# Four graph layers on one core: the queries of the last two layers through a replicated DRAM table, the lock of the slow work released, the row fetch of layer 0 moved

## The chip, the core and the metric

The kernel runs on one core of a Trainium2 chip. The metric is the device time of one execution in microseconds (us). Every time below comes from the runs of the kernel before or from one profiled execution of it.

## The reference, cut to what matters

Sixteen graphs share one adjacency matrix of 1024 nodes with about 8 neighbours for each node. Node features are 128 numbers in float32. Four layers follow each other; layers 0, 2 and 3 are attention with 8 heads of 16 numbers, layer 1 is a graph attention with one head.

```python
# layers 0, 2, 3
Q = (h @ Wq); K = (h @ Wk); V = (h @ Wv)          # 8 heads of 16
scores = einsum(Q, K) / 4, -inf where adj == 0
attn_out = softmax(scores) @ V
x = layer_norm(h + attn_out @ Wo + bo)
x = layer_norm(x + relu(x @ W1 + b1) @ W2 + b2)
# layer 1
h = x @ W;  e = leaky(h @ a_src [:, None] + h @ a_dst [None, :]), -inf where adj == 0
x = layer_norm(softmax(e) @ h + x)
```

## The kernel before, in words

Nodes are sorted by their number of neighbours, and the sparse rows are gathered. The 16 graphs are handled as two groups `g` of eight, and each group as two halves `h` of four. A **unit** is a layer `l`, a group `g` and a tile `t` of 128 sorted nodes; there are 4 x 2 x 8 = 64 units, run in that order. For each unit the neighbours are taken in rounds: a chunk is 32 nodes with four neighbours each, on 128 partitions, so a gathered row sits on partition 32 s + n for neighbour s of node n. Two chunks (in layer 1 four) make a **part**. In layers 0, 2 and 3 the units t = 0 to 7 have 10, 6, 6, 6, 4, 4, 4 and 3 parts; in layer 1 they have 6, 3, 3, 3, 2, 2, 2 and 2.

One part i of an attention layer passes through these functions:

- `gathered` (L750): indirect DMAs from POOL fetch table rows (keys and values of eight graphs, 8 KB a row) into `e`. Four buffers exist, and parts are fetched three ahead.
- `products` (L761): DVE multiplies keys by `qr`, the queries of the unit repeated on all four groups of 32 partitions.
- `exponentials` (L777, L781): DVE sums over each head, ACT takes the exponential.
- `weighted` (L802): DVE multiplies values by `ex`.
- `summed` (L829): PE adds the neighbours up into `acc`.
- `divided` (L843 to L861), at a unit's end: sums of exponentials, reciprocal, division; it appends two **tails**, one for each half.

A tail (`attention_tail`, `graph_tail`) runs the rest of the layer for 128 nodes of four graphs: output projection, two normalizations (`normed`, with ACT L502 and L511 and the power on POOL L508), the feed-forward part, and `finish`. In `finish` the result is turned (`turned`, L518) into `xn`, stored to the DRAM tensor `kept`, and projected by `project` to the table rows of the next layer (L460, L464, store L469; into layer 1 L480 to L495). Tails are Python generators; each `yield` is a point where other work can be placed.

Every engine runs its instructions in the order in which the Python program emits them; a hand-written schedule sets it. The main loop emits one part after the other and calls `others()` three times for a part (four times in layer 1). A call advances the tails at a pace of `STEPS` steps for a unit (`GRAPH_STEPS` after layer 1), and one step of `fronts`, or, if that is empty, of `slow`:

- `fronts` holds `queries(u + 1)` and `loaded(u + 2)`, put there at the second part of a unit and used up by its end. `queries` multiplies x by Wq (L722), copies the result to `q` (L726), repeats it on the four groups of partitions by matmuls with the constant `rep` (L731), and copies it to `qr` (L734). `qr` has two buffers. `loaded` fetches x for the unit after next: from `kept` on SP's queue, in layer 0 by an indirect DMA of `in_x` (L693) and a transposition (L518).
- `slow` holds `at_leisure(1)`: the projection of group 1 of the input for layer 0, 16 tiles `xg` of 128 nodes and four graphs. It has to be done before unit (0, 1, 0) is gathered.

`finish` and `at_leisure` both use the two `xT` buffers, and two flags keep them apart. `busy` counts tails that are in `finish`; `held` is true while `at_leisure` is within a tile. `finish` begins with

```python
            while held[0]:
                advance(slow)
```

and `at_leisure` sets `held[0] = False` after a tile and then goes straight on to the next one, where it sets `held[0] = True` before its next `yield`.

Weights of the next attention layer are loaded at the start of the unit t = 1 of group 0 (`load_weights`, two sets of buffers). SP issues all DMAs that are not indirect, in program order; POOL issues the indirect ones.

Of the kernel before, what the change touches and what calls it, by code (L numbers as in the profile page):

```python
# [12 lines left out]
F32 = mybir.dt.float32  # L13
# [7 lines left out]
P = 128  # L21
D = 128
# [20 lines left out]
GR = 2  # L43
# [17 lines left out]
            CHUNK[_t, _r, _j] = len(CHUNK)  # L61
NC = len(CHUNK)

STEPS = 15
GRAPH_STEPS = 9
AHEAD = 3

# [9 lines left out]
def sparse_path(ctx: ExitStack, tc: tile.TileContext, a: dict, out: bass.AP, flag):  # L77
# [358 lines left out]
    for l, (_, names) in enumerate(LAYERS):  # L436
# [5 lines left out]
        (l, g): dram.tile([T, P, HF, GH * P], F32, name=f"kept{l}{g}")  # L442
        for l in range(1, len(LAYERS)) for g in range(GR)
    }
    xs = {}
    srcs = {}


    def project(l, g, t, h, x, kv=None):

        if l:
            nc.sync.dma_start(kept[l, g][t, :, h, :], x.rearrange("p g n -> p (g n)"))
        table = tables[l, g][t * P : (t + 1) * P, :]
        if LAYERS[l][1] is ATTN:
            if kv is None:
                kv = twos.tile([P, 2, GH, D], F32, tag="kv", name="kv")
            for i in range(0, GH, 2):
                ps = bank([P, 2, 2 * D])
                for k in range(2):
                    nc.tensor.matmul(  # L460
                        ps[:, k, :], x[:, i + k, :], w[LAYERS[l][0], "Wkv"],
                        start=True, stop=True,
                    )
                nc.scalar.copy(  # L464
                    kv[:, :, i : i + 2, :].rearrange("p c g d -> p g c d"),
                    ps.rearrange("p g (c d) -> p g c d", d=D),
                )
                yield
            nc.sync.dma_start(  # L469
                table.rearrange("p (c x) -> p c x", c=2)[:, :, h * GH * D : (h + 1) * GH * D],  # L470
                kv.rearrange("p c g d -> p c (g d)"),
            )
            return
        kv = twos.tile([P, GH * D + GH], F32, tag="kv", name="kv")
        if h == 0:
            srcs[g, t] = const.tile([P, G], F32, name=f"src{g}{t}")
        for i in range(0, GH, 2):
            ps = bank([P, 2, D + 2])
            for k in range(2):
                nc.tensor.matmul(ps[:, k, :], x[:, i + k, :], wg, start=True, stop=True)  # L480
            nc.scalar.copy(
                kv[:, i * D : (i + 2) * D].rearrange("p (g d) -> p g d", d=D), ps[:, :, :D]
            )
            to = GH * D + i
            nc.scalar.copy(
                kv[:, to : to + 2].rearrange("p (g o) -> p g o", o=1), ps[:, :, D : D + 1]
            )
            at = h * GH + i
            nc.scalar.copy(
                srcs[g, t][:, at : at + 2].rearrange("p (g o) -> p g o", o=1), ps[:, :, D + 1 :]  # L490
            )
            yield

        nc.sync.dma_start(table[:, h * GH * D : (h + 1) * GH * D], kv[:, : GH * D])
        nc.sync.dma_start(table[:, ROW + h * GH : ROW + (h + 1) * GH], kv[:, GH * D :])  # L495
# [31 lines left out]
    def finish(l, g, t, h, z, gain, shift):  # L527
        if l + 1 < len(LAYERS):

            while held[0]:  # L530
                advance(slow)
            busy[0] += 1
            xn = states.tile([P, GH, P], F32, tag="xT", name="xT")
            turned(z, xn, gain, shift)
            yield
            yield from project(l + 1, g, t, h, xn)
            busy[0] -= 1
            return
        o = twos.tile([P, GH, D], F32, tag="kv", name="outs")
        nc.gpsimd.tensor_tensor(o, z, over_graphs(gain), ALU.mult)  # L540
        nc.gpsimd.tensor_tensor(o, o, over_graphs(shift), ALU.add)
        nc.gpsimd.indirect_dma_start(
            out=out.rearrange("n (k c) -> (n k) c", k=GR * HF),
            out_offset=bass.IndirectOffsetOnAxis(ap=places[:, g, h, t : t + 1], axis=0),
            in_=o.rearrange("p g d -> p (g d)"), in_offset=None,
        )
# [66 lines left out]
        at = (g * HF + h) * GH * D  # L613
        return slice(at, at + n * GH * D)

    busy, held = [0], [False]

    def at_leisure(g):
        def fetch(k):
# [10 lines left out]
        for k in range(T * HF):  # L630
# [4 lines left out]
            yield  # L635
            yield from steps
            held[0] = False

    def at_once(g):

# [40 lines left out]
    def loaded(u):  # L681
# [5 lines left out]
        if l == 0:  # L687
            for h in range(HF):
# [6 lines left out]
                    in_=a["x"].rearrange("n (k c) -> (n k) c", k=GR * HF),  # L695
                    in_offset=bass.IndirectOffsetOnAxis(ap=places[:, g, h, t : t + 1], axis=0),
                )
                yield
                turned(rows, xs[units[u]][:, h])
            yield  # L700
            return
# [5 lines left out]
    def queries(u):  # L707

        l, g, t = units[u]
        if not is_attention(u):  # L710
# [4 lines left out]
            nc.scalar.copy(ofs[u], ps)  # L715
            return
        qs[u] = reps.tile([P, J, ROW], F32, tag="qr", name="qr")
        for h in range(HF):
            q = ones_.tile([P, GH * D], F32, tag="q", name="q")
            ps = bank([P, GH, D])  # L720
# [143 lines left out]

    tails = []
    fronts = []
    slow = []

    def advance(gens):
# [9 lines left out]
    def others():  # L879
        pace[0] += pace[1]  # L880
        while pace[0] >= 1.0:
            advance(tails)
            pace[0] -= 1.0
        for gens in (fronts or idle(),):
            if gens and next(gens[0], "end") == "end":
                gens.pop(0)

    with tc.manual_schedule():
        wide = [gather_buffer() for _ in range(AHEAD + 1)]
# [34 lines left out]
        for i in range(len(parts) + 1):  # L924
# [30 lines left out]
                pace[:] = 0.0, steps / (passes * sum(part[0] == u for part in parts) - 1)  # L955
            if here and u + 1 < len(units):
                if i == begun + 1:
                    fronts.append(queries(u + 1))
                    fronts.append(loaded(u + 2))
                    if units[u + 2 : u + 3] and units[u + 2][0]:  # L960
                        for _ in fronts.pop():
                            pass
            others()
            if here and is_attention(u):
                exponentials(i)
# [450 lines left out]
```

## Time and profile before

| | |
|---|---|
| median of 3 runs | 2901.22 us (2899.43 to 2903.95) |
| profiled execution, its own time | 2907.46 us |
| its span in the profile | 2905.7 us |
| busy: PE, DVE, ACT, POOL | 72%, 71%, 50%, 53% |
| DMA moved | 611.00 MB, 210 GB/s |
| queue q0 (indirect), q1 (SP) | 485.12 MB, 123.51 MB |
| layer 0, layer 1 (from the first part) | 96 to 956 us, 956 to 1349 us |
| layer 2, layer 3 | 1349 to 2094 us, 2094 us to the end |

Stages are read from the timeline of DVE: a unit begins with its first `products` (L761), in layer 1 with its first L783. In a line of waits the columns are the waiting instruction, what it waited for, the sum in us, how often, and the longest. In a line of the timeline they are start, duration, engine, line, operation and shapes, and in brackets the idle time of the engine ahead of it and what ended that. A busy share is a mean over stages with different limits, so the windows by stage matter more than the totals.

### The profile page before, as it was taken

The numbers are of one execution on the slowest core, as the hardware profiler recorded it, in microseconds if no ns is written. First come the engines' busy times: TensorE is split into PE (matmuls) and PEld (weight loads), VectorE is DVE, ScalarE is ACT, GpSimd is POOL, SyncE is SP. The second block draws the span as 40 slices with busy tenths as digits, with TensorE's granted clock in tenths as the row PEclk, the third lists the DMA queues.
The fourth block names the chain that finished last, engine by engine and source line by source line (L and its number), as shares of the span: only waits on it lengthen the run. The fifth ranks groups of instructions, "written<-read, shape, count | busy, mean of one in ns | idle before, by whom it ended". The sixth has DMA issues, their size and how long they took to land.

```text
span 2905.7 us, 35508 instructions
## 1 busy us (share of the span) xinstructions
PE 2101.5 (72%) x12692; PEld 1310.9 (45%) x12692; DVE 2076.4 (71%) x1416; ACT 1458.6 (50%) x4578; POOL 1542.7 (53%) x1096
## 2 busy tenths in 40 slices
PE   6456777777777867766578877887777776757666
PEld 5334544444454534333245544554544444334444
DVE  7872585678776566667788659886688876888771
ACT  3133555644566545445256664556645455435554
POOL 3342354354554687784254334544346767586773
PEclk8687888887798988888688998889988788887787
DMA  7656464357464577787567546675566554366540
GB/s 248 249 194 213 158 240 164 135 189 271 166 258 141 194 275 270 267 288 290 194 235 264 193 176 253 237 266 192 186 235 229 199 218 168 140 249 213 189 146 20
DMA packets 168842, 611.00 MB, mean 210 GB/s; under 512 B 44600, under 2 KB 47672, under 8 KB 120158
## 3 DMA queue, kind: packets, MB, share of 16 engines
q0 software_dynamic: 100736, 485.12, 46.4%
q1 hardware_dynamic: 67920, 123.51, 11.6%
q8 instruction: 102, 1.67, 0.2%
q14 instruction: 84, 0.69, 0.1%
HBM read 654.67 MB, written 92.34 MB: 257 GB/s over the span
## 4 chain that ended last, share of the span: by engine, by line
PE 26%; POOL 13%; ACT 11%; DVE 9%; issue 8%; DMA 3%; POOLq 0%; SPq 0%; DVEq 0%; ACTq 0%
POOL e L750 6%; PE ps L572 5%; PE yps L581 4%; PE acc L829 4%; POOL rstd L508 4%; DVE sc L777 3%; ACT z L502 3%; PE ps L518 3%; DMA e<-table,idx 2%; ACT qr L734 2%; DVE pr L802 2%; PE yps L585 2%; PE ps L460 2%; DVE pr L761 2%; PE yps L562 2%
## 5 line engine op out<-in xcount | busy, mean ns | idle before, releaser
L750 POOL DMA_INDIRECT e<-table,idx x656 | 908.4, 1385 | 343.6 <-issue 164.3
L802 DVE TENSOR_TENSOR pr<-e,ex 128x2048 f32<-128x2048 f32 (+1 forms) x344 | 760.6, 2218 | 452.7 <-ACT ex L781 445.0
L508 POOL TENSOR_TENSOR rstd<-total,power 128x4 f32<-128x4 f32 x224 | 370.8, 1656 | 654.4 <-ACT z L502 635.5
L761 DVE TENSOR_TENSOR pr<-e,qr 128x2048 f32<-128x2048 f32 (+1 forms) x258 | 565.4, 2192 | 128.0 <-DMA e<-table,idx 69.7
L829 PE MATMUL acc<-pr,marks 128*32 128x512 f32 x2624 | 475.3, 708 | 131.3 <-DVE pr L802 122.8
L777 DVE TENSOR_REDUCE sc<-pr 128x128 f32<-128x2048 f32 (+1 forms) x258 | 562.2, 2179 | 0.0
L518 PE MATMUL ps<-ident,z 128*128 128x128 f32 x768 | 178.6, 344 | 186.4 <-ACT z L511 183.6
L502 ACT ACTIVATE z<-yps,root 128x128 f32<-128x128 f32 x768 | 272.6, 384 | 70.7 <-PE yps L585 68.3
L581 PE MATMUL yps<-W,f 128*128 128x128 f32 x1536 | 261.4, 288 | 21.9 <-ACT f L576 18.6
L829 PEld LDWEIGHTS acc<-pr,marks 128*32 128x32 f32 x2624 | 90.2, 122 | 399.2 <-issue 223.8
L511 ACT ACTIVATE z<-yps,rstd 128x128 f32<-128x128 f32 x768 | 222.4, 391 | 80.4 <-POOL rstd L508 79.7
L518 PEld LDWEIGHTS ps<-ident,z 128*128 128x128 f32 x768 | 116.3, 163 | 323.7 <-ACT z L511 228.9
L572 PE MATMUL ps<-x,W 128*128 128x512 f32 x384 | 221.8, 708 | 41.7 <-ACT x L522 41.7
L460 PE MATMUL ps<-Wkv,xT 128*128 128x256 f32 x768 | 227.8, 444 | 27.9 <-ACT xT L522 17.4
L581 PEld LDWEIGHTS yps<-W,f 128*128 128x128 f32 x1536 | 213.4, 197 | 76.3 <-ACT f L576 52.0
L576 ACT ACTIVATE f<-ps,b 128x512 f32<-128x512 f32 x192 | 131.4, 687 | 213.5 <-PE ps L572 213.2
L731 PE MATMUL ps<-q,rep 32*128 32x512 f32 x768 | 177.3, 701 | 80.9 <-ACT q L726 41.6
L781 ACT ACTIVATE ex<-sc 128x128 f32<-128x128 f32 (+1 forms) x258 | 81.6, 316 | 289.5 <-DVE sc L777 289.5
L734 ACT COPY qr<-ps 128x512 f32<-128x512 f32 x384 | 197.9, 601 | 42.1 <-PE ps L731 40.5
L460 PEld LDWEIGHTS ps<-Wkv,xT 128*128 128x128 f32 x768 | 157.0, 217 | 72.0 <-ACT xT L522 27.5
L561 PE MATMUL yps<-Wo,oT 128*128 128x128 f32 x768 | 178.5, 319 | 7.4 <-ACT oT L520 7.4
L562 PE MATMUL yps<-centre,x 128*128 128x128 f32 x768 | 173.4, 312 | 4.6
(146 smaller groups left out, 2799.6 us busy)
## 6 DMA issues: line engine op xcount, KB each, us to landing
table<-kv SPq DMA_DIRECT2D x88, 512.0 KB, 7.2
kept<-xT SPq DMA_DIRECT2D x96, 256.0 KB, 4.9
x<-kept SPq DMA_DIRECT2D x48, 512.0 KB, 10.5
e<-table,idx POOLq DMA_INDIRECT x656, 7.5
table<-kv SPq DMA_DIRECT2D x32, 256.0 KB, 5.1
edges<-in_adj SPq DMA_DIRECT2D x8, 512.0 KB, 5.7
spare<-in_x SPq DMA_DIRECT2D x8, 512.0 KB, 6.6
table<-ex SPq DMA_DIRECT2D x8, 512.0 KB, 5.8
```

The source lines that it names most:

```text
L460: nc.tensor.matmul(ps[:, k, :], x[:, i + k, :], w[LAYERS[l][0], "Wkv"], start=True, stop=True,)
L502: nc.scalar.activation(z[:, i, :], y[:, i, :], AF.Square, scale=D**-0.5, bias=root, accum_out=total[:, i : i + 1],)
L508: nc.gpsimd.tensor_tensor(rstd, total, power, ALU.pow)
L518: nc.tensor.transpose(ps[:, i, :], z[:, i, :], ident)
L572: nc.tensor.matmul(ps, p["W1"][:, f * P : (f + 1) * P], x1.rearrange("p g n -> p (g n)"), start=True, stop=True,)
L581: nc.tensor.matmul(ps[:, i, :], f1[:, f, i * P : (i + 1) * P], p["W2"][:, f, :], start=(f == 0), stop=False,)
L734: nc.scalar.copy(qs[u][:, j, h * GH * D : (h + 1) * GH * D], pss[j])
L750: nc.gpsimd.indirect_dma_start(out=es[i][:, k, :], out_offset=None, in_=tables[l, g][:, :], in_offset=bass.IndirectOffsetOnAxis(ap=idx[:, ...
L761: nc.vector.tensor_tensor(prs[i][0][:, :n, :], es[i][:, :n, :ROW], qs[u][:, j : j + n, :], ALU.mult)
L777: nc.vector.tensor_reduce(sc[:, :n, :], prs[i][0][:, :n, :].rearrange("p k (a d) -> p k a d", d=HD), mybir.AxisListType.X, ALU.add,)
L802: nc.vector.tensor_tensor(prs[i][k0 // 2][:, :m, :].rearrange("p k (a d) -> p k a d", d=d), es[i][:, k0 : k0 + m, base : base + ROW].rearr ...
L829: nc.tensor.matmul(accums[u][32 * j : 32 * j + 32, h, :], marks[:, CHUNK[t, r, j], :], tiles[j // 2][:, j % 2, h * GH * D : (h + 1) * GH * D],
```

## The change

`STEPS` becomes 16. The lock: `finish` sets a flag `wanted` while it advances `slow`, and `at_leisure` yields once after a tile when the flag is set. The fetch: `loaded` goes to a list of its own, `loads`, which `others()` turns to when `fronts` is empty; in layer 0 it yields `"idle"` twice after the indirect DMA, and at such a yield `others()` also advances `slow`. From layer 1 on, where x comes from `kept`, the load is issued at once, ahead of the queries.

The queries: `project` for layers 2 and 3 also multiplies by Wq, copies the result to a staging tile `q` (tag `y`, two buffers, the tag of `y` in `graph_tail`) and stores it to a DRAM table `qtab` with a row of 4 KB for each node. `queries` in layers 2 and 3 then holds no PE or ACT instruction: it issues 16 DMAs from SP, for each of four chunks four loads of the same 32 rows, one to each group of 32 partitions of `qr`. Layer 0 makes its queries as before.

```diff
-STEPS = 15
+STEPS = 16
...
+    qtabs = {
+        (l, g): dram.tile([N, ROW], F32, name=f"qtab{l}{g}")
+        for l, (_, names) in enumerate(LAYERS) if l and names is ATTN for g in range(GR)
+    }
...
@@ project, after the store of the table rows
+            if l:
+                q = twos.tile([P, GH * D], F32, tag="y", name="q")
+                ps = bank([P, GH, D])
+                for i in range(GH):
+                    nc.tensor.matmul(
+                        ps[:, i, :], x[:, i, :], w[LAYERS[l][0], "Wq"], start=True, stop=True
+                    )
+                nc.scalar.copy(q, ps.rearrange("p g d -> p (g d)"))
+                yield
+                nc.sync.dma_start(
+                    qtabs[l, g][t * P : (t + 1) * P, h * GH * D : (h + 1) * GH * D], q
+                )
...
@@ finish
+            wanted[0] = True
             while held[0]:
                 advance(slow)
+            wanted[0] = False
...
@@ at_leisure
             yield from steps
             held[0] = False
+            if wanted[0]:
+                yield
...
@@ loaded, layer 0
-                yield
+                yield "idle"
+                yield "idle"
                 turned(rows, xs[units[u]][:, h])
...
@@ queries
         qs[u] = reps.tile([P, J, ROW], F32, tag="qr", name="qr")
+        if l:
+            for j in range(J):
+                at = t * P + 32 * j
+                rows = qtabs[l, g][at : at + 32, :]
+                for s in range(S):
+                    nc.sync.dma_start(qs[u][32 * s : 32 * s + 32, j, :], rows)
+            return
...
@@ others
-        for gens in (fronts or idle(),):
-            if gens and next(gens[0], "end") == "end":
+        for gens in (fronts or loads or idle(),):
+            if not gens:
+                continue
+            got = next(gens[0], "end")
+            if got == "end":
                 gens.pop(0)
+            if got == "idle":
+                advance(idle())
...
@@ main loop
                 if i == begun + 1:
+                    while loads:
+                        advance(loads)
                     fronts.append(queries(u + 1))
-                    fronts.append(loaded(u + 2))
+                    loads.append(loaded(u + 2))
                     if units[u + 2 : u + 3] and units[u + 2][0]:
-                        for _ in fronts.pop():
-                            pass
+                        advance(loads)
```

## The prediction

> **What bounds the kernel now.** I read the slices of the page first, then the windows by stage, then the waits of each stage, and last the timeline at the longest wait.
>
> ```profile
> DVE  7872585678776566667788659886688876888771
> ...
> DMA  7656464357464577787567546675566554366540
> ```
>
> No engine is full for the whole span. DVE reaches 8 or 9 in layers 2 and 3 and drops to 2 in the fourth slice (218 to 291 us). The windows below are the drain around that hole, the rest of layer 0 by group, layer 1, and layers 2 and 3 by group; the columns are busy us of PE, PEld, DVE, ACT and POOL, granted clock, DMA share and GB/s.
>
> ```profile
> 247.00:312.00 65.00, 39.04 (x151) 27.97 (x154) 0.34 (x1) 22.44 (x48) 1.20 (x1) 0.79 0.53 192
> 312.00:572.00 260.00, 197.71 (x1248) 127.66 (x1240) 178.52 (x95) 151.79 (x495) 118.46 (x87) 0.84 0.50 178
> ...
> 956.00:1349.00 393.00, 291.05 (x1948) 164.42 (x1948) 242.82 (x264) 184.54 (x631) 296.79 (x214) 0.86 0.75 262
> 1349.00:1726.00 377.00, 275.83 (x1628) 166.83 (x1632) 290.97 (x165) 202.29 (x609) 158.85 (x120) 0.84 0.61 224
> ```
>
> From 247 to 312 us DVE does 0.34 us of work. In layer 2, DVE works 291 of 377 us and PE 276: units of six parts are close to DVE's time, the short ones (three or four parts) wait for the tails. Layer 1 is held by gathers: POOL 297 of 393 us, DMA share 0.75. The timeline of DVE shows what ends the hole, and the next fences the waits over the span and, of DVE, in 1349 to 2094 us (layer 2) and 2094 to 2811 us (layer 3 without its end).
>
> ```profile
> 245.06 2.28 DVE L761 TENSOR_TENSOR pr<-e,qr 128x2048 f32<-128x2048 f32 x1
> 312.01 2.29 DVE L802 TENSOR_TENSOR pr<-e,ex 128x2048 f32<-128x2048 f32 x1 [64.67 <-ACT ex L781]
> ```
>
> ```profile
> DVE pr L802 <- ACT ex L781: 445.0, 109, 64.7
> ...
> PE ps L518 <- DMA rows<-in_x,places: 74.6, 20, 7.3
> ```
>
> ```profile
> DVE pr L802 <- ACT ex L781: 117.1, 37, 8.4
> DVE pr L761 <- ACT qr L734: 21.0, 2, 11.9
> ```
>
> ```profile
> DVE pr L802 <- ACT ex L781: 63.2, 23, 8.5
> DVE pr L761 <- DMA e<-table,idx: 53.3, 19, 5.6
> DVE pr L761 <- ACT qr L734: 25.1, 2, 13.2
> ```
>
> The exponential L781 is 0.32 us of work; DVE waits for it because ACT runs in order and has tail and query work ahead of it that waits for PE. The 64.7 us are one such wait: `finish` (L530) emits all that `at_leisure` has left ahead of that exponential, because `held` becomes False and True again between two yields. In the program's order 13 of the 16 tiles of group 1 stand there.
>
> **What the Trainium skill says.** "SBUF — State Buffer", section "Door 1: The DMA port swizzle", gives a transfer into partitions 0 to 31 eight of sixteen ports and 189 GB/s at 1 MiB. Each of the new loads fills 32 partitions. No transfer of the trace before has that shape: its 128-partition queue q1 moved 123.51 MB in 11.6% of 16 engines' span, 366 GB/s while moving. "DMA: Bandwidth & Descriptors", section "Issuing engines are not separate DMA queues", says that DMAs of SP and POOL share the same 16 engines; the trace agrees: q0 of POOL and q1 of SP are both counted on those 16 engines (46.4% and 11.6% of their span). Section "Anatomy of one DMA" puts about 2 us of fixed time on each; here 128 KB weights land after 2.2 us and 256 KB of `xg` after 3.7 us (median).
>
> **The change part by part.** The profiled execution took 2907.5 us (span 2905.7 and 1.8 around it), 6 us over the median of the runs; the sum is made on 2907.5 and 6 are taken off at the end.
>
> 1. Lock. In the changed order four slow tiles stand in unit 0 and two in each of units 1 to 6, none later. The hole goes, less the 2.5 us that a usual wait of this kind takes (445.0 - 64.7 over 108 is 3.5; beside this one 2.2): 62 us. The work stays: a tile is 0.63 us of transposes and 1.99 us of L460 on PE, and three copies of 0.59 us on ACT, so 12 tiles put 31 us of PE and 21 us of ACT into units 1 to 6. The window 312 to 572 has 62 us free on PE and 108 on ACT, which covers it if it falls into gaps; but ACT and PE in order are just what DVE waits for there, so I charge 20 (0 if all is hidden, 49 if each tile costs its 4.1 us of the drain in full). **-42**, from -13 to -62. Next late: the same exponential, by 2 to 4 us at a time.
>
> 2. Fetch. The row gathers of layer 0 (landing 3.5 us median) now go behind the queries and two more calls of `others`, in which a slow step is emitted instead. PE's 74.6 us of waits for rows should go nearly all; 50.2 of them lie in 312 to 956 us. Only what passes through ACT to the exponential counts: half, **-25**, from 0 to -50. POOL's wait for the row buffer (L693, 84.6 us) moves later but stays; POOL is at half load there and hides it. STEPS 16 raises the pace of tails by 1/15 and adds no instruction: 0, from -5 to +5.
>
> 3. Layer 1 pays for the queries of layer 2: 16 units, each 8 matmuls 128x128 (16 records, 1.8 us at the 1.77 us that eight records took), two copies of 0.59 us and two stores of 256 KB from SP. 8.4 MB at 366 GB/s are 23 us of DMA where the share is 0.75. The tail gets one more step, in units of two parts whose tails run to the end of the unit anyway. The staging buffers have the tag of `y` (L598): DVE's addition for the next unit waits until the store of the unit before has landed, and DVE's next part waits behind it; table stores of 256 KB take 5.1 us. **+15**, from 0 (hidden) to +45 (23 of DMA and 1.4 us a unit for the buffer).
>
> 4. Layers 2 and 3 lose, in each of 32 units, 8 matmuls 32x512 (16 records, two groups of 1.1 to 1.5 us, 2.5 us of PE) and 8 copies L734 of 0.60 us, 4.8 us of ACT. Wq matmuls and query copies leave layer 3; in layer 2 those for layer 3 take the place of its own. In layer 2 the waits to be shortened are 117 us for the exponential and 21 for qr (the units after the three-part units). Of the 138, ACT's relief of 16 x 4.8 = 77 us can reach at most 77; I take half, **-40** (-15 to -75). In layer 3, 88 us of such waits, but POOL and gathers stand next (53.3 us): **-20** (0 to -50).
>
> 5. What it adds there. Sixteen loads of 128 KB for each unit, 67.1 MB in all, and 64 stores of 256 KB (16.8 MB), half of them counted in 3. 2.1 MB for a unit are 5.7 us at 366 GB/s, 11 us at the skill's 189 (an estimate), and about 16 us beside gathers that take half of the engines, with two fixed times. SP issues a load in about 0.4 us (xg), so 6.4 us at least; it may have eight under way, each further one waits for the one eight before it. They are issued at the second part of a unit and wanted at the next unit, two to nine parts of 7.7 us later; behind them on SP stand only kept, table and query stores, half a unit from their need. So I cost the loads at nothing on DVE, the cover being the 15 us of a three-part unit. Gathers running meanwhile land later by up to their own 7.5 us; they are issued three parts ahead (23 us), but layer 3 already waits for them: **+12**, 0 to +60. The first two products of a unit wait for up to eight more semaphores; PE's semaphore instructions in the trace take 51 ns, so 16 x 0.05 x 32 is 26 us at most, mostly ahead of the engine: **+8**, 0 to +26.
>
> Sum: -42 - 25 + 15 - 40 - 20 + 12 + 8 = -92. 2907.5 - 92 is 2815; less 6, **2810 us** at the level of the median.
>
> **Rivals.**
> A. The lock and fetch work, the table gives nothing: contention and layer 1 eat parts 4 and 5. For it: the DMA share of 0.6 in layer 2 and the waits for e in layer 3. Against: ACT's qr waits are in the trace, 57.0 us over the span. -67 + 15 + 20 = -32: about 2870.
> B. The slow tiles only move: each costs its 4.1 us again (-13), while the rest goes as forecast: -63, about 2838.
> C. Slower: the query loads come too late. DVE's first product of a unit waits for all loads of its pair of rows, and behind it stands the whole part. Against: the 15 to 60 us of cover. It begins at a load time of about 15 us in three-part units and 23 in four-part units (two and three parts of 7.7 us), and decides where it eats the 92 us. If the loads take 30 us beside gathers, the 3 boundaries after three-part units lose 15 each and the 12 after four-part units 7 each, 129 us: +37 over all, about 2939.
> D. The change doesn't do what it says: the order of instructions shows that it does, so only 2 in 100.
>
> **How the numbers follow.** Forecast 55, A 15, B 15, C 12, others 3 in 100. A difference under 0.2% (6 us) is about what a measurement of this kernel can't tell from none. Taking all good ends would give 2670, all bad ends about 3000; a spread of some 65 us each way around the sum holds the forecast's own cases, A and B lie inside, and half of C outside: 2740 to 2893. Faster 0.83, within 0.2% 0.05, slower 0.12.
>
> **What would show it.** Step 1: no DVE wait over 20 us in layer 0, slow transposes two in each unit. Step 2: PE's wait for rows under 20 us. Step 3: layer 1 longer than 393 us by 5 to 30. Step 4: qr waits on ACT gone in layers 2 and 3, layer 2 in 350 us a group. Step 5: DVE waiting for DMA qr would make C right; a wait of DVE for e above 53 us in layer 3 would show the contention. A total above 2893 or a layer 2 longer than before would make the prediction wrong.

## The result, and the profile after

| | before | after |
|---|---|---|
| median of 4 runs | 2902.59 us (2899.43 to 2905.27) | 2951.30 us (2942.89 to 2955.92) |
| span of the profiled execution | 2905.7 us | 2941.1 us |
| layers 0, 1, 2, 3 | 860, 393, 745, 811 us | 787, 460, 742, 856 us |
| busy PE, DVE, ACT, POOL | 72%, 71%, 50%, 53% | 69%, 71%, 45%, 51% |

The ratio is 1.0165 (1.0139 to 1.0191): the kernel is 48 us slower, where 92 us less were forecast. The layers are read from DVE's first instruction of each, as before. Layer 0 lost 73 us, layer 1 gained 67, layer 2 lost 3 and layer 3 gained 45. The work has shrunk as the change says (ACT from 50% to 45%); the waits have grown. The slices of the page after:

```profile
DVE  7877755787774645656697677877777776778772
...
DMA  7657654565645766767798897989977677576750
```

The hole in DVE's fourth slice is gone. DVE in layer 1 (slices 13 to 18), at 5 and 6 before, is now at 4 to 6 and stays there longer, and DMA in slices 21 to 29 (layer 2) is at 7 to 9 where it was at 4 to 7. The windows of layer 0, layer 1, the first group of layer 2, and a stretch of 396 us in layer 3, with the columns of before (busy us of PE, PEld, DVE, ACT and POOL, granted clock, DMA share, GB/s):

```profile
96.00:883.00 787.00, 587.35 (x3615) 386.88 (x3615) 589.70 (x404) 422.15 (x1361) 360.57 (x264) 0.85 0.59 214
883.00:1343.00 460.00, 318.35 (x2137) 189.48 (x2136) 241.34 (x262) 195.07 (x654) 276.40 (x217) 0.82 0.71 246
1343.00:1719.00 376.00, 263.93 (x1518) 169.83 (x1519) 290.93 (x164) 169.91 (x534) 164.08 (x117) 0.83 0.85 271
2085.00:2481.00 396.00, 247.90 (x1392) 152.96 (x1391) 299.25 (x154) 152.17 (x525) 225.98 (x158) 0.79 0.74 240
```

The first group of layer 2 needs 376 us as it did before (377), although ACT does 32 us less in it and PE 12 us less; the DMA share went from 0.61 to 0.85. In layer 1 DVE works the same 241 us in 67 us more. The waits name what came in between. First those of DVE over the whole span:

```profile
DVE pr L832 <- ACT ex L811: 321.7, 88, 12.4
DVE y L618 <- DMA qtab<-q: 117.1, 21, 13.4
DVE pr L791 <- DMA e<-table,idx: 89.2, 27, 6.8
DVE pr L791 <- DMA qr<-qtab: 82.8, 14, 11.6
```

The wait for the exponential fell from 445.0 to 321.7 us and its longest from 64.7 to 12.4. The waits on ACT for `qr` (57.0 us before) remain only in layer 0. In their place stand two waits that did not exist: 117.1 us for a `y` buffer whose `qtab` store has not landed, and 82.8 us for the query loads. Of the first, 116.7 us lie in layer 1. Ahead of the same products stand another 29.6 us for which the profile shows no cause (before: 1.1 us); the landing of about half of the loads is not in the trace, so part of these may be waits for loads too. The waits of DVE in 2085 to 2844 us, layer 3 without its end:

```profile
DVE pr L832 <- ACT ex L811: 66.6, 20, 6.9
DVE pr L791 <- DMA e<-table,idx: 59.4, 15, 6.8
DVE pr L791 <- DMA qr<-qtab: 32.2, 6, 11.5
```

Before, these were 63.2 (exponential), 53.3 (gathers) and 25.1 us (`qr` from ACT): nothing has fallen.

Two timelines show the new waits. DVE in layer 1:

```profile
1045.67 0.69 DVE L618 TENSOR_TENSOR y<-o,yps 128x512 f32<-128x512 f32 x1 [10.03 <-DMA qtab<-q]
```

An addition of 0.69 us stands still for 10 us, because the buffer it writes is still being stored as `q` of another unit. And SP in layer 2, ahead of unit (2, 0, 5), then DVE at the unit's start:

```profile
1577.82 0.43 SPq L725 DMA_DIRECT2D x<-kept  x1
1578.36 26.64 SPq L746 DMA_DIRECT2D qr<-qtab  x16
```

```profile
1595.54 2.28 DVE L807 TENSOR_REDUCE sc<-pr 128x128 f32<-128x2048 f32 x1
1605.01 2.29 DVE L791 TENSOR_TENSOR pr<-e,qr 128x2048 f32<-128x2048 f32 x1 [7.18 <-DMA qr<-qtab]
```

The 16 loads take 26.6 us on SP alone. SP's transfers take turns on eight semaphores, in the trace before as in this one, and each waits until the transfer eight places ahead of it has landed. Here the fourth to the eighth load wait for two table stores, two query stores and the load of `x`; those behind them wait for loads of the same unit. The last landed at 1610.4 us: 32 us for the unit from first issue to last landing. Over the span SP waited for landings as follows ahead of the loads:

```profile
SPq L746 <- DMA qr<-qtab: 157.7, 130, 5.4
SPq L746 <- DMA table<-kv: 99.5, 29, 6.6
SPq L746 <- DMA x<-kept: 71.3, 21, 7.1
SPq L746 <- DMA qtab<-q: 46.2, 33, 3.4
```

So more of this time, 217 us against 158, went to other transfers of SP than to the loads themselves.

### The profile page after: what moved, and what is told of

The parts are those of the page before. It is cut to its first block, busy times and chain, and to the rows that moved or that the text cites. A ratio compares the mean times of both kernels' runs of the same rounds, so it can differ in the third digit from the quotient of the medians.

```text
span 2941.1 us, 35247 instructions
## 1 busy us (share of the span) xinstructions
PE 2037.9 (69%) x12180; PEld 1311.2 (45%) x12180; DVE 2086.2 (71%) x1416; ACT 1330.4 (45%) x4322; POOL 1493.0 (51%) x1096
## 3 DMA queue, kind: packets, MB, share of 16 engines
q1 hardware_dynamic: 101712, 207.43, 22.4%
## 4 chain that ended last, share of the span: by engine, by line
PE 25%; DMA 17%; issue 10%; ACT 9%; DVE 9%; POOL 8%; POOLq 0%; DVEq 0%; SPq 0%; ACTq 0%
DMA e<-table,idx 7%; PE ps L591 4%; PE yps L600 4%; DMA qtab<-q 4%; POOL e L780 3%; ACT z L519 3%; PE ps L535 3%; PE acc L859 3%; DMA qr<-qtab 3%; PE ps L465 3%; DVE sc L807 3%; DVE pr L791 3%; DVE pr L832 3%; POOL rstd L525 2%; PE yps L581 2%
## 5 line engine op out<-in xcount | busy, mean ns | idle before, releaser
L780 POOL DMA_INDIRECT e<-table,idx x656 | 921.4, 1405 | 383.5 <-DVE pr L832 193.4
L832 DVE TENSOR_TENSOR pr<-e,ex 128x2048 f32<-128x2048 f32 (+1 forms) x344 | 764.1, 2228 | 327.4 <-ACT ex L811 321.7
L791 DVE TENSOR_TENSOR pr<-e,qr 128x2048 f32<-128x2048 f32 (+1 forms) x258 | 573.0, 2221 | 239.0 <-DMA e<-table,idx 89.2
L525 POOL TENSOR_TENSOR rstd<-total,power 128x4 f32<-128x4 f32 x224 | 316.8, 1415 | 768.8 <-ACT z L519 752.2
L535 PE MATMUL ps<-ident,z 128*128 128x128 f32 x768 | 185.0, 341 | 197.5 <-ACT z L528 196.8
L465 PE MATMUL ps<-Wkv,xT 128*128 128x256 f32 x768 | 234.9, 447 | 31.7 <-ACT xT L539 20.3
L580 PE MATMUL yps<-Wo,oT 128*128 128x128 f32 x768 | 199.8, 351 | 73.6 <-ACT oT L537 73.6
L591 PE MATMUL ps<-x,W 128*128 128x512 f32 x384 | 208.6, 670 | 37.5 <-ACT x L539 37.5
L535 PE MATMUL ps<-ident,o 128*128 128x128 f32 x384 | 82.1, 353 | 180.1 <-DVE o L883 179.2
L580 PEld LDWEIGHTS yps<-Wo,oT 128*128 128x128 f32 x768 | 154.8, 250 | 110.9 <-ACT oT L537 94.7
L581 PE MATMUL yps<-centre,x 128*128 128x128 f32 x768 | 197.1, 347 | 5.0
## 6 DMA issues: line engine op xcount, KB each, us to landing
qtab<-q SPq DMA_DIRECT2D x64, 256.0 KB, 10.2
```

Of the source, the lines that this page charges most:

```text
L465: nc.tensor.matmul(ps[:, k, :], x[:, i + k, :], w[LAYERS[l][0], "Wkv"], start=True, stop=True,)
L525: nc.gpsimd.tensor_tensor(rstd, total, power, ALU.pow)
L535: nc.tensor.transpose(ps[:, i, :], z[:, i, :], ident)
L580: nc.tensor.matmul(ps[:, i, :], oT[:, i, :], p["Wo"], start=True, stop=False)
L591: nc.tensor.matmul(ps, p["W1"][:, f * P : (f + 1) * P], x1.rearrange("p g n -> p (g n)"), start=True, stop=True,)
L780: nc.gpsimd.indirect_dma_start(out=es[i][:, k, :], out_offset=None, in_=tables[l, g][:, :], in_offset=bass.IndirectOffsetOnAxis(ap=idx[:, ...
```

## The experiments

All ratios are to the kernel before on the same chip. Differences between kernels are taken from the ratios and told in us of 2903 (the median before); layers are those of one profiled execution each, and good to some 10 us: four kernels with the same program in layer 0 (`lock_fetch`, `after_15`, `own_15`, `own_noloads_15`) show 775 to 793 us there. Two theories were tried first: the loads and their buffers hold DVE up, or the lock and fetch do not bring what was forecast. Later ones have letters in the expectations: **I**, the number of issues makes the loads late; **P**, PE's granted clock falls when it has less to do; **O**, the tail's place ahead of the exponential in ACT's order makes DVE wait; its rival **V**, the higher pace itself costs, because the tails end earlier and collide with other work.

| kernel | ratio (95%) | layers 0, 1, 2, 3 in us |
|---|---|---|
| after | 1.0165 (1.0139 to 1.0191) | 787, 460, 742, 856 |
| lock_fetch | 0.9757 (0.9731 to 0.9784) | 775, 393, 749, 813 |
| fetch_only | 0.9846 (0.9817 to 0.9875) | 812, 387, 745, 813 |
| own_staging | 0.9981 (0.9967 to 0.9995) | 787, 415, 745, 850 |
| four_loads | 1.0380 (1.0352 to 1.0409) | 789, 476, 782, 861 |
| own_noloads | 0.9894 (0.9853 to 0.9934) | 792, 434, 718, 847 |
| own_quarter | 0.9894 (0.9861 to 0.9927) | 790, 428, 725, 846 |
| own_warm | 1.0040 (1.0025 to 1.0055) | 791, 425, 749, 856 |
| noloads_warm | 0.9907 (0.9880 to 0.9935) | 786, 424, 731, 841 |
| lock_fetch_16 | 1.0044 (1.0027 to 1.0061) | 795, 401, 780, 846 |
| after_15 | 0.9958 (0.9938 to 0.9978) | 793, 455, 755, 814 |
| own_15 | 0.9812 (0.9753 to 0.9871) | 779, 415, 749, 814 |
| own_noloads_15 | 0.9708 (0.9688 to 0.9727) | 784, 412, 711, 814 |
| swap_16 | 1.0320 (1.0285 to 1.0355) | 832, 404, 802, 867 |
| swap_15 | 0.9987 (0.9973 to 1.0001) | 809, 394, 749, 832 |
| lock_fetch_14 | 0.9726 (0.9693 to 0.9759) | 771, 391, 730, 823 |
| delay_16 | 0.9961 (0.9944 to 0.9979) | 796, 391, 758, 844 |
| early_15 | 1.0227 (1.0198 to 1.0257) | 818, 401, 784, 870 |

### The lock and the fetch without the table

`lock_fetch` is the kernel before with the lock and the fetch of the diff and nothing else: queries by matmuls, `STEPS` 15.

> The kernel before with the lock and the fetch alone, STEPS 15, no query table. Theory S (the parts are separate: lock and fetch gain the 73 us that layer 0 lost between the two traces, the table costs 108 us in layers 1 to 3): about 2830 us, ratio 0.975, layer 0 in 787 us, layers 1 to 3 within 6 us of before each. Rival B of the prediction (the slow tiles only move): layer 0 above 820 us and 2860 us or more. If the changed order of layer 0 also bears on layer 1, layer 1 is longer than 393 us by more than 5.

`fetch_only` leaves the lock out as well.

> The kernel before with the fetch alone: the rows go behind the queries with two idle steps, the lock as before, so the hole of 64.7 us stays or is moved. My estimate of the parts in the prediction: fetch -25 of 67, lock -42, so about 2877 us (ratio 0.991). If the lock is all of the gain: 2900 us. If the fetch is most of it: below 2860.

Measured: lock and fetch give -71 us, all in layer 0 (860 to 775). The fetch alone gives -45 and the lock on top of it -26. With the fetch alone the drain is shorter but still there, as one line of DVE's waits in 95 to 907 us of `fetch_only` shows by its longest wait:

```profile
DVE pr L803 <- ACT ex L782: 183.3, 39, 48.5
```

So the mechanism of steps 1 and 2 and their sum are right, with the shares the other way round in this order. The lock without the fetch was not tried, so how much of the drain belongs to which of them is not shown. And whatever makes the changed kernel slow lies in the table or in `STEPS`.

### The staging buffers

```diff
-                q = twos.tile([P, GH * D], F32, tag="y", name="q")
+                q = ones_.tile([P, GH * D], F32, tag=("q", "xg")[h], name="q")
```

In `own_staging` `q` has two buffers of its own, apart from `y`.

> The changed kernel, but the query staging tiles of the halves 0 and 1 take two buffers of their own, which layer 0 used and which are free afterwards, instead of sharing the two y buffers. Theory Y (in layer 1 DVE's y waits for the staging stores): the wait of y for qtab stores (117 us) goes, layer 1 falls from 460 to 400-415 us, and the total to about 2890-2905 (ratio to before about 1.00). Rival D (layer 1 is longer by the 8.4 MB of stores, whatever the buffer): layer 1 stays above 440 us, the total above 2925.

Measured: -53 us, of which layer 1 gives 45 (460 to 415). DVE's waits in its layer 1 (882 to 1298 us):

```profile
DVE y L618 <- PE yps L615: 48.8, 15, 4.9
DVE sc L813 <- DMA e<-table,idx: 48.3, 19, 6.8
```

The wait for the store is gone; the same addition now waits for PE, and the gathers are next. The gain is 45 us of the 116.7 that the wait had, because these two take over. At `STEPS` 15 the same edit gives -42 us (`after_15` against `own_15`).

### The query loads

```diff
-            for j in range(J):
-                at = t * P + 32 * j
-                rows = qtabs[l, g][at : at + 32, :]
-                for s in range(S):
-                    nc.sync.dma_start(qs[u][32 * s : 32 * s + 32, j, :], rows)
+            rows = qtabs[l, g][t * P : (t + 1) * P, :].rearrange("(j n) c -> n j c", n=32)
+            for s in range(S):
+                nc.sync.dma_start(qs[u][32 * s : 32 * s + 32, :, :], rows)
```

`four_loads` moves the same bytes in 4 DMAs of 512 KB instead of 16 of 128 KB.

> The changed kernel, but the queries of a unit come in 4 DMAs of 512 KB (32 partitions x 4 rows of 4 KB each) instead of 16 of 128 KB: the same bytes, a quarter of the issues, never more than eight under way. Theory I (the loads are late because SP issues sixteen with eight under way, 14 to 27 us from first to last): the last load lands within 12-15 us, DVE's waits for qr (82.8 us) fall under 20, layers 2 and 3 gain 40-60 us: about 2895. Rival W (the loads are late for the bytes and the 32 partitions, they take the same DMA time): the last landing and the waits stay as they are, total within 10 us of 2951.

`own_noloads` is `own_staging` with the loads of 30 of the 32 units left out: from the third unit of layer 2 on, `qs[u]` is the tile of two units before. `own_quarter` makes all 16 loads in these 30 units, with a quarter of the columns, into that same tile.

> own_staging, but the query loads are issued for the first two units of layer 2 alone; all later units of layers 2 and 3 multiply by these old queries (this leaves out 30 of 32 query loads; the tables are still stored). Theory L (the relief of ACT and PE is worth what I forecast, and the loads eat it): layer 2 falls from 745 to 690-710 us and layer 3 from 850 to 780-800, total about 2790-2800. Rival P (the relief is worth nothing, since PE with less work is granted a lower clock and its chain takes as long): the waits for qr go, 60 and 40 us, but layer 3 stays at 820 us or more with a granted clock under 0.80, total above 2830.

> own_staging, but after the first two units of layer 2 each of the 16 loads brings a quarter of the columns (1 KB of 4 KB a row; the rest of the queries is old): the same number of issues and waits, a quarter of the bytes. If the bytes are the cost: within 10 us of own_noloads. If the number of DMAs, eight under way, is the cost: within 10 us of own_staging (2893 us), and the last load still lands more than 15 us after the first issue.

Measured: fewer and larger loads are worse, +62 us over the changed kernel. The waits of DVE in `four_loads` over the span:

```profile
DVE pr L789 <- DMA e<-table,idx: 147.7, 42, 9.1
...
DVE pr L789 <- DMA qr<-qtab: 107.0, 8, 21.9
```

Both waits rose, that for the gathers from 89.2 to 147.7 us and that for the loads from 82.8 to 107.0. The edit changed two things, though: the first product of a unit needs two of the four chunks, which are the first eight of the 16 loads, but all four of the large ones. What each of the two costs was not tried apart. Leaving the loads out gives -25 us (0.9981 to 0.9894), and layer 2 falls from 745 to 718; layer 1, where little was left out, shows 434 us instead of 415, for which no cause is shown. A quarter of the bytes at the full number of issues gives the same -25. Theory I fell: with all the issues the time falls when the bytes do, as far as without loads, and with a quarter of the issues it does not fall. It is the bytes, next to the gathers and to SP's other transfers.

But even without loads the kernel stood at 0.9894, above the 0.9757 of the lock and fetch alone, and layer 3 was still at 847 us. So the loads are not the main cause.

### PE's granted clock

In layer 3 the granted clock is 0.77 in the changed kernel (2085 to 2844 us) and 0.83 in the one before. `own_warm` puts the matmuls with `rep` back into `queries`, their results unused; `noloads_warm` does that without the loads.

```diff
+            for h in range(HF):
+                yield
+                for j in range(J):
+                    ps = bank([P, GH * D])
+                    nc.tensor.matmul(ps, rep_of(j), xs[l, g, t][32 * j : 32 * j + 32, h]..., start=True, stop=True)
+                yield
```

> own_staging, with the 8 matmuls 32x512 of the former replication put back for each unit of layers 2 and 3 at their former place, their result unused: only PE's work is put back, no copies on ACT. Theory P (the lower granted clock of layer 3, 0.78 against 0.82, costs): the clock of layer 3 returns to 0.81 or more and layer 3 is shorter by 10 us or more. Theory L: PE only gets more to do, layers 2 and 3 are longer by 0 to 30 us.

> own_noloads with the same unused matmuls: neither loads nor copies, but PE's former work (30 of 32 query loads are left out). Theory P: layer 3 is shorter than in own_noloads by 10 us or more, at a clock of 0.81 or more. Theory L: longer than own_noloads by 0 to 30 us, and still shorter than the kernel with lock and fetch alone (layer 3 813 us), by what the 8 copies on ACT are worth.

Measured: +17 us with the loads, +4 without, and layer 3 at 856 and 841 us. But the matmuls did not bring the clock back. In layer 3 without its end PE works 510 us in `own_warm` instead of the 456 of `own_staging`, and the clock is 0.79 instead of 0.78; without the loads it is 0.78 with the matmuls and 0.79 without. So these two runs do not test theory P. A pair of the next part does: the windows of layer 3 without its end, first of `own_staging`, then of `own_15`, which differ in `STEPS` alone:

```profile
2043.00:2797.00 754.00, 456.22 (x2564) 276.61 (x2563) 573.63 (x294) 281.36 (x982) 444.05 (x311) 0.78 0.73 236
```

```profile
2038.00:2757.00 719.00, 455.29 (x2555) 281.91 (x2555) 562.19 (x294) 280.40 (x981) 472.47 (x309) 0.77 0.76 245
```

At the same granted clock the layer is 35 us shorter, as short as in `lock_fetch` at 0.83. So the lower clock is not what makes layer 3 longer. Whether it takes back a gain that the layer would have had is not shown.

### STEPS alone

`lock_fetch_16` is `lock_fetch` with `STEPS` 16; `after_15`, `own_15` and `own_noloads_15` are the kernels of those names with `STEPS` 15.

```diff
-STEPS = 15
+STEPS = 16
```

> lock_fetch with STEPS 16 instead of 15 and nothing else. Theory Z (the raised pace puts tail steps at other places ahead of the exponential, which I had costed at nothing): layer 0 goes from 775 to about 787 us as in the changed kernel, layer 3 from 813 to 830-850, total 2860-2890. Rival Q (layer 3 is longer for what the query table does: emptied query steps, e later): layer 3 stays within 5 us of 813, total below 2848.

> The changed kernel with STEPS 15 and nothing else. Theory Z: layer 0 falls from 787 to about 775 us, layer 3 from 856 to 815-835, and layer 1 keeps its waits for the staging stores (460 us): total about 2900-2915, level with before. Rival Q: only layer 0 gets shorter, total about 2939. In layer 2 the tails have a step more than in before, so a pace of 15 leaves one more to be drained at the unit's end: 0 to +15 us there.

> own_staging with STEPS 15. Theory Z: about 2845-2865 us (layer 0 775, layer 1 415, layer 3 815-835), so still slower than lock_fetch (2832), as the query loads cost what the relief gives. Rival Q: 2880.

> own_noloads with STEPS 15 (30 of 32 query loads left out). What the relief of ACT and PE is worth without loads and with the old pace: by my forecast 40 us in layer 2 and 20 in layer 3 against lock_fetch, so layer 2 about 705-715 and layer 3 about 790, total about 2800. If relief is worth nothing: layer 2 at 740, layer 3 at 813, total about 2850 (layer 1 stays longer than 393).

Measured: this one number costs 83 us without the table (0.9757 to 1.0044) and 60 us in the changed kernel (0.9958 to 1.0165). Layer 3 shows it in every pair: 846 and 813, 856 and 814, 850 and 814, 847 and 814. The price of the table depends on `STEPS` in turn: with buffers of its own it costs 16 us at 15 (0.9757 to 0.9812; the interval of `own_15` is 17 us to each side) and gains 18 us at 16 (1.0044 to 0.9981). One line of DVE's waits over the span, first of `lock_fetch`, then of `lock_fetch_16`:

```profile
DVE pr L807 <- ACT ex L786: 351.0, 104, 8.9
```

```profile
DVE pr L807 <- ACT ex L786: 437.0, 110, 13.8
```

The wait for the exponential rises by 86 us, as much as the time. What stands ahead of the exponential in ACT's order is seen in unit (2, 0, 2), which went from 46.4 to 50.8 us. ACT's timeline there, first of `lock_fetch`:

```profile
1436.29 0.69 ACT L578 ACTIVATE f<-ps,b 128x512 f32<-128x512 f32 x1 [0.17 <-PE ps L574]
1436.88 0.30 ACT L786 ACTIVATE ex<-sc 128x128 f32<-128x128 f32 x1
1437.08 0.36 ACT L502 ACTIVATE z<-yps,root 128x128 f32<-128x128 f32 x1
```

and of `lock_fetch_16`:

```profile
1468.08 0.69 ACT L578 ACTIVATE f<-ps,b 128x512 f32<-128x512 f32 x1 [0.17 <-PE ps L574]
1468.66 0.36 ACT L502 ACTIVATE z<-yps,root 128x128 f32<-128x128 f32 x1
...
1469.94 0.22 ACT L502 ACTIVATION_READ_ACCUMULATOR z<-yps,root 128x1 f32 x1
1470.03 0.33 ACT L786 ACTIVATE ex<-sc 128x128 f32<-128x128 f32 x1
```

At the higher pace a step of the normalization L502 has moved ahead of the exponential, which starts 1.4 us later after the same L578. No instruction was added.

The pair at `STEPS` 15 also gives the table's parts. DVE's waits in layer 2 of `own_15` (1289 to 2038 us), then of `own_noloads_15` (1296 to 2007 us):

```profile
DVE pr L791 <- DMA qr<-qtab: 77.8, 10, 15.6
DVE pr L832 <- ACT ex L811: 36.8, 21, 3.7
```

```profile
DVE pr L836 <- ACT ex L815: 99.5, 34, 10.0
...
DVE pr L795 <- DMA qr<-qtab: 16.0, 1, 16.0
```

Without the loads layer 2 needs 711 us instead of 749: the relief of ACT and PE is there, 38 us against `lock_fetch`. With the loads it is 749 again. The wait of 16.0 us in the second view, like one of 15.6 in the first, still lies in layer 1, and `own_15` has one of 13.9 us ahead of the first unit of layer 3. Counted so, the waits for `qr` are 76 us longer with the loads and those for the exponential 63 us shorter; longer waits for gathers (18.0 against 9.3 us) and 12.5 us without a cause in the profile make up most of the rest of the 38. In layer 3 neither kernel moves from 814.

### Which place in the order

If the place of a tail's steps between the calls is the cause (theory O), and not the higher pace (V), it should show at an unchanged pace too. `swap_16` and `swap_15` are `lock_fetch_16` and `lock_fetch` with the exponential emitted ahead of the second call of `others`:

```diff
-            others()
             if here and is_attention(u):
                 exponentials(i)
+            others()
```

`lock_fetch_14` has `STEPS` 14. `delay_16` is `lock_fetch_16` with one more empty step at the head of an attention tail, `early_15` is `lock_fetch` with the pace counter starting at 1 in attention units, so that every step comes up to a call earlier:

```diff
-        for _ in range(h):
+        for _ in range(h + 1):
```

```diff
-                pace[:] = 0.0, steps / ...
+                pace[:] = float(is_attention(parts[begun - 1][0])), steps / ...
```

> lock_fetch_16 with one call of others moved: the exponential of a part is emitted ahead of the second of its three calls, not behind it. Theory O (what costs 86 us at STEPS 16 is the place of single tail steps: in the units of six parts a normalization's first half, 8 instructions on ACT, comes ahead of the exponential instead of behind it): the order of ACT changes, DVE's waits for the exponential fall from 437 us to 350 or less and the total to 2830-2860. Rival V (the higher pace itself: tails end earlier and collide with queries and gathers): the total stays above 2890.

> lock_fetch with the same call moved, STEPS 15. Theory O: with less work of ACT ahead of each exponential the waits for it fall below 351 us, total 2800-2835; or another step is put ahead of it and it loses up to 30 us. Rival V: no change, 2832 within 8.

> lock_fetch with STEPS 14. Theory O: the place of the steps decides, not the pace: any result from 2810 to 2890 and no line through 14, 15 and 16. Rival V: a lower pace is better still or the same, below 2832, by up to as much as 16 was worse (86 us).

> lock_fetch_16 with one empty step more at the head of each attention tail: the pace of STEPS 16 stays, but every tail step comes one call later. In the second half of a unit of six parts the steps then stand at the calls that they have at STEPS 15. Theory O (the place of the steps, not the pace): total 2825-2850. Rival V (the pace): total above 2890.

> lock_fetch, STEPS 15, with the pace's counter starting at 1 instead of 0 after attention units: the pace of 15 stays, but every tail step comes one call earlier, so that the second half of a unit of six parts stands as at STEPS 16, with the normalization's first half ahead of the exponential. Theory O: total 2885-2930. Rival V: total 2825-2845.

Measured: the swap makes both slower, by 80 us at 16 and 67 at 15. DVE's waits in `swap_16` over the span:

```profile
DVE pr L807 <- ACT ex L786: 346.2, 93, 11.3
DVE pr L766 <- DMA e<-table,idx: 163.1, 43, 9.6
DVE pr L766 <- ACT qr L739: 83.8, 5, 19.0
DVE both L855 <- ACT both L853: 78.6, 27, 14.1
```

The wait for the exponential falls to the level of `lock_fetch`, as O expected, but the gathers, the queries and the divisions wait instead. O in its simple form, "get the exponential ahead and the time is back", fell.

The others shift tail steps and leave the exponential where it is. DVE's wait for it over the span, in `lock_fetch_14`, `delay_16` and `early_15`:

```profile
DVE pr L807 <- ACT ex L786: 353.9, 111, 10.1
```

```profile
DVE pr L807 <- ACT ex L786: 428.0, 120, 8.5
```

```profile
DVE pr L807 <- ACT ex L786: 475.3, 127, 14.0
```

With the 351.0 and 437.0 above, these five kernels have the same order by this wait and, but for the first two, by their time: 353.9, 351.0, 428.0, 437.0 and 475.3 us beside ratios of 0.9726, 0.9757, 0.9961, 1.0044 and 1.0227. At one rate of steps to a call, steps up to a call earlier cost 136 us (`early_15`), which theory V had put at nothing; and a step later at 16 gives 24 back (`delay_16`). So where the steps stand between the calls can cost more than the raised pace did, with no instruction added.

That the pace costs nothing for itself is not shown. `delay_16` had to come below 2850 us by theory O and above 2890 by V, and came at 2894; `lock_fetch_14`, at 2821, lies where both theories had put it. And in `early_15` the tails end earlier as well, so it does not part a step's place from an earlier end of the tails.

Which step it is stays open. The sums of unit lengths in layer 2 from the trace:

| kernel | units of six parts | units of four parts |
|---|---|---|
| lock_fetch_14 | 287.4 us | 213.1 us |
| lock_fetch | 279.3 us | 232.3 us |
| delay_16 | 268.6 us | 242.8 us |
| lock_fetch_16 | 296.5 us | 235.9 us |
| early_15 | 273.4 us | 260.5 us |

From 15 to 16 over half of the loss of layer 2 is in the units of six parts, and `delay_16` wins it back there; but `early_15`, the slowest, has short units of six parts too and loses in those of four. So a shift that is good for units of one length can be bad for those of another.

Of the kernels that leave nothing out, **lock_fetch_14** is the fastest here, at 2821.2 us; it beats both kernels and has no table. Its lead over `lock_fetch` (0.9726 against 0.9757) is within their intervals.

## Why the prediction was wrong

The measured parts beside those on record, in us. The table's parts are taken at `STEPS` 15 and the pace last. Totals are differences of ratios times 2903, and the two with `own_15` are good to some 17 us; those marked "layer" are differences of layers in two profiled executions, and good to some 10 us.

| step | forecast | measured | by |
|---|---|---|---|
| 1 and 2, lock and fetch | -67 | -71 | `lock_fetch` against before |
| 2, `STEPS` 16 | 0 | +60 | after against `after_15` |
| 3, queries made in layer 1 | +15 with the buffers | +19 (layer) | `own_noloads_15` against `lock_fetch` |
| 3, buffers with the tag of `y` | in the +15 | +42 | `after_15` against `own_15` |
| 4, layer 2 | -40 | -38 (layer) | `own_noloads_15` against `lock_fetch` |
| 4, layer 3 | -20 | +1 (layer) | the same pair |
| 5, loads, gathers, semaphores | 0 + 12 + 8 | +30 | `own_15` against `own_noloads_15` |
| all | -92 | +48 | after against before |

The measured terms add up to 43. In another order they would be others, since the price of the table depends on the pace.

**Steps 1 and 2 were right in lock and fetch.** No wait of DVE in layer 0 is over 20 us (the longest is 11.9, on `qr` from ACT), and PE's waits for rows fell from 74.6 to 28.5 us, which is less of a fall than the "under 20" on record. That fetch and lock came to 71 where 67 were forecast is partly luck: alone, the fetch gave 45 instead of 25, and the lock on top of it 26 instead of 42.

**The step that failed most is the sentence on STEPS in step 2**: "raises the pace of tails by 1/15 and adds no instruction: 0, from -5 to +5". It counted instructions. Step 1 of the same text names the mechanism, ACT in order with tail work ahead of the exponential, and did not apply it to the pace. Without the table the term is +83. That tail steps come ahead of exponentials, and that DVE waits longer for them, is shown; whether the pace costs beyond that stays open.

**Step 3 was mis-sized**. Layer 1 became 67 us longer, not 15. The buffer term was 1.4 us a unit, 22 us, from a store of 256 KB that lands in 5.1 us; it cost 42 to 53. The DMA issues on the page after (KB each, median us to landing) have twice that time, over all stores; for those of layer 1 alone the trace has 8.5 us:

```profile
qr<-qtab SPq DMA_DIRECT2D x512, 128.0 KB, 9.5
...
qtab<-q SPq DMA_DIRECT2D x64, 256.0 KB, 10.2
```

What is left of layer 1 without most of the loads is +19, near the +15, but not for the reason given. DVE's wait for the `yps` of PE rose from 30.1 us in `lock_fetch` to 45.9 in `own_noloads_15`, and the wait ahead of the first unit of layer 2 from 9.1 to 16.0, while that for the gathers fell from 55.9 to 50.0: this points to work on PE in the tails, and not to the DMA of the stores.

**Step 4 was right in layer 2 and wrong in layer 3.** The relief of layer 2 is 38 us where 40 were forecast, seen only when the loads are left out; that half of ACT's 77 us would reach DVE was a guess that came out. In layer 3 it is 0 where 20 were forecast. There the wait for `qr` (25.2 us in `lock_fetch`) is gone in `own_noloads_15`, but the waits for gathers went from 54.2 to 62.1 us and those for the exponential from 63.2 to 67.4. "POOL and gathers stand next (53.3 us)" was in the text; that they took all of the gain is not shown. PE's granted clock in this layer is also lower, 0.79 instead of 0.83, and whether that had a part in it stays open.

**Step 5 failed on the cover.** The loads were put at about 16 us and hidden behind 15 us of a three-part unit; they took 20 to 34 us from the first issue to the last landing that the trace has in layer 2, and cost 30. The text knew the limit of eight transfers but counted only the loads against it; the stores and the load of `x` ahead of them on SP took turns too, for the 217 us shown above. "SBUF — State Buffer" of the Trainium skill, section "Door 1: The DMA port swizzle", had been used for 189 GB/s into 32 partitions. Here the added 83.9 MB of q1 (loads and stores) took 322 us of 16 engines (22.4% of 2941.1 less 11.6% of 2905.7), 261 GB/s: less than the 366 of before; no run here shows these loads alone. With a quarter of the bytes the cost was gone, so the estimate of 16 us, half of the engines and two fixed times, was too low by a half. (The section from which the prediction took 2 us of fixed time speaks of DMAs issued from GpSimd. These loads are SP's; for SP the trace before has 2.2 us for 128 KB of weights, landing included.) "DMA: Bandwidth & Descriptors" of the Trainium skill, section "Rules for kernel authors", advises one large transfer instead of many small ones; here 512 KB against 128 KB was slower by 62 us, beside gathers and with the first product waiting for all of the unit's bytes; how much of that is the size alone is not shown. The +12 for later gathers did not show in layer 3, which had 814 us with and without the loads. The 8 us for semaphores were not measured apart.

Two sizes in the working were off without bearing on this: 16 records at 1.77 us for eight are 3.5 us and not 1.8 (measured after: 2.2 us for a unit), and the matmuls with `rep` took 3.7 us of PE for a unit before, not 2.5. The good ends of all terms add up to some 2660 us, not 2670.

**Rivals.** C, with its 30 us for a unit's loads and 2939 us, comes near the total and has the load time right, the total by luck. But its price was 129 us and the loads cost 30; the buffers and the pace, 42 and 60, made up the total, and no rival named the pace. A was right that contention eats the relief of layer 2. B did not happen: on top of the fetch, the lock removed a wait of 48.5 us (some 46 more than usual) and gave 26, 37 by layer 0, so the moved tiles cost 9 to 20 us, about the 20 charged in step 1. The range ended at 2893 since it held only half of C and nothing for the pace.

## What to carry to other kernels

In a program whose engines run in order, a constant that sets where independent work is placed is part of the change and has to be priced, to begin with by what it puts ahead of the instruction that the bound engine waits for: here one step more in fifteen cost 83 us, more than the lock and fetch brought. Price a buffer that is shared with a store by the store's landing time in the changed kernel, which was 8.5 to 10.2 us here against the 5.1 of a like store before. Count all transfers of a queue against its limit, not only the new ones. When a wait is removed, its gain is what the next one leaves: in layer 2 the loads took back the 38 us that the relief of ACT and PE gave, and in layer 3 no gain was seen even without them.

## What was not expected of the hardware

Sixteen loads of 128 KB beside indirect gathers cost less than four of 512 KB with the same bytes: DVE's wait for gathers went from 89.2 to 147.7 us with the larger ones, and the longest wait for the queries from 11.6 to 21.9 us. Part of the second may come from the first product's need for all four. And PE's granted clock in layer 3 fell from 0.83 to 0.77 without being what made the layer longer: at 0.77 and `STEPS` 15 the layer took 814 us (`own_15`), at 0.78 and 16 it took 850 (`own_staging`). Putting unused matmuls back, 54 us of work of PE, did not bring the clock back either (0.78 to 0.79).
